# Attention probabilities transposed by VectorE in 32x32 blocks and DMA, with each group's queries projected one group ahead

## The chip, the cores and the metric

The kernel runs on one core of one Trainium2 chip. The metric is the device time of one launch in microseconds, the median of several runs. All data are fp32.

## What is computed

The input is a tensor of 2 images, 128 channels, 64 x 64 pixels. It goes through four layers: a state-space layer (layer 0), two attention layers over all 4096 pixels of an image (layers 1 and 2), and a multi-scale layer with attention over four scales at each pixel (layer 3). The change lies in layers 1 and 2, which are:

```
# layer 1: q, k, v are 3x3 convolutions of x, n = h * w = 4096
attn = softmax(einsum('bci,bcj->bij', q, k) * c ** -0.5, axis=2)
out  = einsum('bij,bcj->bci', attn, v).reshape(b, c, h, w)
x    = x + conv2d(out, Wo, bo, 0)
# layer 2: q, k, v are 1x1 projections of x
attn = softmax(einsum('nci,ncj->nij', q, k), axis=-1)
x    = gamma[0] * einsum('ncj,nij->nci', v, attn) + x
```

## The kernel before

Both images stay in SBUF the whole time, in `xt`, with channels on the 128 partitions and a border of zeros round each image. Layer 0 has an order of instructions written out by hand. From the attention layers on, the tile framework's scheduler chooses the order of each engine's instructions when the program is built, from the program's order and the buffers that each pool has. On every engine the instructions then run in that fixed order: one that waits holds back what stands behind it.

The two attention layers share the function `attention`, which is called once for each layer and image, four times in all. `project` and `finish` are given by the caller: `project` is the nine taps of a convolution in layer 1 (L633) and one product in layer 2 (L648); `finish` adds the result to `xt` (L638 after the output projection L637, or L651).

A call first projects the keys, the values and the queries of the whole image, 512 pixels at a time, into PSUM tiles `pp` of two chunks; ScalarE adds the bias and writes `k` and `q` (L572) or `vs` (L575). Values are transposed by PE (L579) and copied by VectorE (L581) to `vt`, which has keys on the partitions.

Then it goes through the queries in 16 groups of QG = 256, each in two blocks `it` of 128 queries:

- PE multiplies the block's queries with all keys (L594), into PSUM tiles `pq` of 1024 keys, of which there are two buffers. VectorE copies each to `sc` and takes the maximum on the way (L596).
- VectorE makes the negative scaled maximum `nm` (L598, L599), ScalarE takes the exponential of the whole row of 4096 in place and sums it (L601), and VectorE takes the reciprocal of the sum to `rec` (L602).
- `sc` has queries on the partitions, and the product with the values needs keys there. PE transposes it in 128 x 128 squares, four to a PSUM bank `ptt` (L607), and VectorE copies each bank to `pt` (L608). The eight `pt` tiles of a group have one of ten buffers each.
- When both blocks are there, PE sums the 32 products of `vt` with `pt` (L611) to `po`. The reciprocals are spread over the partitions by a product of ones with a diagonal matrix `dg` (L616, L617), copied by ScalarE to `rb` (L619), and multiplied in (L621).

The DMA queue of SyncE (SP) issues all transfers. In the attention layers it has only the loads of weights. DMAs are counted by eight semaphores in turn, so an issue waits until the DMA eight before it has landed. Each fp32 product is two passes of PE in the profile (so L594 counts 2048 and L611 4096 instructions); a transpose is one.

Of the kernel before, what the change touches and what calls it, by code (L numbers as in the profile page):

```python
# [6 lines left out]
F32 = mybir.dt.float32  # L7
AF = mybir.ActivationFunctionType
# [5 lines left out]
B, C, H, W = 2, 128, 64, 64  # L14
N = H * W
P = 128
CH = 512
NCH = N // CH
RPC = CH // W
# [39 lines left out]
WS_O, WS_Q, WS_K, WS_V, WS_IN, WS_OUT, WS_FUS = 0, 128, 256, 384, 512, 896, 1024  # L59
# [4 lines left out]
def tile_conv_seq(ctx: ExitStack, tc, x, consts, vecs, wemb, wlay, wconv, wdt, wqkv, wsmall, wms, out):  # L64
    nc = tc.nc
# [5 lines left out]
    ws = kp.tile([P, NWS], F32, name="ws")  # L71
    xt = kp.tile([P, B, H + 2, W + 2], F32, name="xt")
# [5 lines left out]
    def xv(b, c):  # L78

        return xt[:, b, 1 + c * RPC : 1 + (c + 1) * RPC, 1 : W + 1]  # L80
# [13 lines left out]
    ident = kc[:, K_ID : K_ID + P]  # L94
# [40 lines left out]
    with ExitStack() as s, tc.manual_schedule():  # L135
        wp = s.enter_context(tc.tile_pool(name="l0w", bufs=1))
        sp = s.enter_context(tc.tile_pool(name="l0s", bufs=1))
# [25 lines left out]
        for l in range(NL):  # L163
            w = wp.tile([P, NWL], F32, name=f"wl{l}")
# [12 lines left out]
            a = wp.tile([P, NJ, 4, 4], F32, name=f"am{l}")  # L177
            for g in range(4):
                pa = mm.tile([P, NJ, DS], F32, name="pa", tag="mm")
                nc.tensor.matmul(pa.rearrange("p j n -> p (j n)"), lhsT=four(g), rhs=an, start=True, stop=True)  # L180
                for q in range(4):
                    at = slice(32 * q, 32 * q + 32)
# [344 lines left out]
        for i in range(-2, NI + 2):  # L527
            todo = background(i)
            for t_ in range(NSL):
                t = i * NSL + t_  # L530
# [18 lines left out]
    wq = wbig.tile([P, 3, 9, C], F32, name="wq", tag="wbig")  # L549
    nc.sync.dma_start(wq, wqkv)  # L550
    nc.sync.dma_start(ws, wsmall)
    QG = 256
    with ExitStack() as s:
        sp = s.enter_context(tc.tile_pool(name="ats", bufs=1))
        pss = s.enter_context(tc.tile_pool(name="atps", bufs=2, space=PSUM))
        pst = s.enter_context(tc.tile_pool(name="atpt", bufs=2, space=PSUM))
        psa = s.enter_context(tc.tile_pool(name="atpa", bufs=1, space=PSUM))
        psm = s.enter_context(tc.tile_pool(name="atpm", bufs=1, space=PSUM))

        def attention(b, project, biases, scale, finish):  # L560

            q = sp.tile([P, N], F32, name="q", tag="q")
            k = sp.tile([P, N], F32, name="k", tag="k")
            vt = sp.tile([P, N // P, C], F32, name="vt", tag="vt")
            for which in (1, 2, 0):
                for c2 in range(NCH // 2):
                    pp = pss.tile([P, 2, CH], F32, name="pp", tag="s")
                    for i in range(2):
                        project(which, 2 * c2 + i, pp[:, i, :])
                    if which < 2:  # L570
                        dst = (q, k)[which][:, c2 * 2 * CH : (c2 + 1) * 2 * CH].rearrange("p (a f) -> p a f", a=2)
                        nc.scalar.activation(dst, pp, AF.Identity, bias=biases[which])  # L572
                        continue
                    vs = sp.tile([P, 2, CH], F32, name="vs", tag="vs", bufs=1)
                    nc.scalar.activation(vs, pp, AF.Identity, bias=biases[which])  # L575
                    for i in range(2):
                        pt = pst.tile([P, 4, P], F32, name="pvt", tag="t")
                        for a in range(4):
                            nc.tensor.transpose(pt[:, a, :], vs[:, i, a * P : (a + 1) * P], ident)  # L579
                        at = (2 * c2 + i) * 4  # L580
                        nc.vector.tensor_copy(vt[:, at : at + 4, :], pt)  # L581

            for grp in range(N // QG):
                pts = [sp.tile([P, 4, QG], F32, name="pt", tag="pt", bufs=10) for _ in range(NCH)]
                rec = sp.tile([P, 2], F32, name="rec", tag="rec", bufs=2)
                for it in range(QG // P):
                    qa = grp * QG + it * P
                    sc = sp.tile([P, N], F32, name="sc", tag="sc", bufs=3)
                    mx = sp.tile([P, NCH // 2], F32, name="mx", tag="mx", bufs=3)
                    for c2 in range(NCH // 2):  # L590
                        pq = pss.tile([P, 2, CH], F32, name="pq", tag="s")
                        for i in range(2):
                            at = (2 * c2 + i) * CH
                            nc.tensor.matmul(pq[:, i, :], lhsT=q[:, qa : qa + P], rhs=k[:, at : at + CH], start=True, stop=True)  # L594
                        dst = sc[:, c2 * 2 * CH : (c2 + 1) * 2 * CH].rearrange("p (a f) -> p a f", a=2)
                        nc.vector.tensor_scalar(dst, pq, 1.0, None, ALU.mult, ALU.max, accum_out=mx[:, c2 : c2 + 1])  # L596
                    nm = sp.tile([P, 1], F32, name="nm", tag="nm", bufs=3)
                    nc.vector.tensor_reduce(nm, mx, AX.X, ALU.max)  # L598
                    nc.vector.tensor_scalar(nm, nm, -scale, None, ALU.mult)  # L599
                    sm = sp.tile([P, 1], F32, name="sm", tag="sm", bufs=3)  # L600
                    nc.scalar.activation(sc, sc, AF.Exp, bias=nm, scale=scale, accum_out=sm)  # L601
                    nc.vector.reciprocal(rec[:, it : it + 1], sm)  # L602
                    for c in range(NCH):
                        pt = pst.tile([P, 4, P], F32, name="ptt", tag="t")
                        for a in range(4):
                            at = c * CH + a * P
                            nc.tensor.transpose(pt[:, a, :], sc[:, at : at + P], ident)  # L607
                        nc.vector.tensor_copy(pts[c][:, :, it * P : (it + 1) * P], pt)  # L608
                po = psa.tile([P, QG], F32, name="po", tag="acc")
                for jt in range(N // P):  # L610
                    nc.tensor.matmul(po, lhsT=vt[:, jt, :], rhs=pts[jt // 4][:, jt % 4, :], start=(jt == 0), stop=(jt == N // P - 1))  # L611

                pr = psm.tile([P, QG], F32, name="pr", tag="m")
                for it in range(QG // P):
                    dg = sp.tile([P, P], F32, name="dg", tag="dg", bufs=2)
                    nc.vector.tensor_scalar(dg, ident, rec[:, it : it + 1], None, ALU.mult)  # L616
                    nc.tensor.matmul(pr[:, it * P : (it + 1) * P], lhsT=ones, rhs=dg, start=True, stop=True)  # L617
                rb = sp.tile([P, QG], F32, name="rb", tag="rb", bufs=2)
                nc.scalar.copy(rb, pr)  # L619
                on = sp.tile([P, QG], F32, name="on", tag="on", bufs=2)  # L620
                nc.vector.tensor_tensor(on, po, rb, ALU.mult)  # L621
                finish(grp, on)

        def xg(b, grp):
            r = QG // W
            return xt[:, b, 1 + grp * r : 1 + (grp + 1) * r, 1 : W + 1]

        for b in range(B):
            def project(which, c, ps, b=b):
                for tap in range(9):  # L630
                    dy, dx = divmod(tap, 3)
                    rhs = xt[:, b, c * RPC + dy : (c + 1) * RPC + dy, dx : dx + W]
                    nc.tensor.matmul(ps, lhsT=wq[:, which, tap, :], rhs=rhs, start=(tap == 0), stop=(tap == 8))  # L633

            def finish(grp, on, b=b):
                p2 = psm.tile([P, QG], F32, name="p2", tag="m")
                nc.tensor.matmul(p2, lhsT=ws[:, WS_O : WS_O + C], rhs=on, start=True, stop=True)  # L637
                nc.vector.scalar_tensor_tensor(xg(b, grp), rows(p2), v1("bo1"), xg(b, grp), ALU.add, ALU.add)  # L638

            attention(b, project, [v1("bq1"), v1("bk1"), v1("bv1")], float(C) ** -0.5, finish)  # L640

        wm = wbig.tile([P, NS, 9, C], F32, name="wm", tag="wbig")
        nc.sync.dma_start(wm, wms)

        for b in range(B):
            def project(which, c, ps, b=b):
                at = WS_Q + which * C
                nc.tensor.matmul(ps, lhsT=ws[:, at : at + C], rhs=xv(b, c), start=True, stop=True)  # L648

            def finish(grp, on, b=b):  # L650
                nc.vector.scalar_tensor_tensor(xg(b, grp), rows(on), v1("gamma"), xg(b, grp), ALU.mult, ALU.add)  # L651

            attention(b, project, [v1("bq2"), v1("bk2"), v1("bv2")], 1.0, finish)


    with ExitStack() as s:
        sp = s.enter_context(tc.tile_pool(name="mss", bufs=1))
# [7 lines left out]
        for si in range(NS):  # L665
            for ti in range(NS):
                r = si * 32 + ti
# [3 lines left out]
        for b in range(B):  # L671
# [3 lines left out]
            for si in range(1, NS):  # L675
                sc_ = SCALES[si]
                hh = H // sc_
# [12 lines left out]
                for r0 in range(0, hh, rn):  # L690
                    pc = mm.tile([P, CH], F32, name="pcs", tag="mm")
                    pcv = pc[:, : rn * hh]
                    for tap in range(9):
                        dy, dx = divmod(tap, 3)
                        nc.tensor.matmul(  # L695
                            pcv, lhsT=wm[:, si, tap, :], rhs=xs[:, r0 + dy : r0 + dy + rn, dx : dx + hh],
# [8 lines left out]
                half = sc_ // 2  # L705
# [187 lines left out]
```

## Time and profile before

| | |
|---|---|
| median of 3 runs | 7203.03 us (7201.87 to 7207.1) |
| the profiled execution | 7203.93 us, its span 7202.1 us |
| mean granted PE clock | 0.912 |
| busy, share of the span | PE 93%, weight load 44%, VectorE 57%, ScalarE 32%, GpSimd 27% |
| layers 1 and 2, from the first `pp` to the last `xt` | 2743.8 to 5473.2 us |
| of these, PE busy | 2717.2 of 2729.4 us |
| DMA | 24.3 MB in the whole span |

A line of the page's part 5 gives a group of instructions: its line in the code, engine, operation, output and inputs, shape and count, then after the bar the busy time in us and the mean of one in ns, and after the second bar the time the engine stood idle just before them and what ended that. A line of instructions in order of time gives the start in us, the duration, engine, line, operation and count, and in brackets the idle time before and its releaser. [...] the distance of two starts tells what one costs in a row. The line PEclk gives the clock that PE was granted, in tenths of full speed, in 40 slices of the span.

### The profile page before, as it was taken

The page shows a single profiled execution, that of the slowest core. Times are in us where ns is not written, and L with a number is a line of the kernel's source. Part 1 is how long each engine was busy: PE and PEld are TensorE (multiplying, and loading weights), DVE is VectorE, ACT ScalarE, POOL GpSimd, SP SyncE. Part 2 cuts the span into 40 slices and gives each one's busy share as a digit, 9 for nine tenths or more (in the row PEclk, how much of TensorE's full clock was granted, in tenths as well). Part 3 has the DMA queues.
Part 4 walks back from the last instruction along what each step waited for, and adds up shares of the span by engine and source line. Part 5 has one row for each costly group of instructions (what it writes and reads, how often), then busy time and mean ns, then how long its engine had stood idle before and what let it go on. Part 6 is the DMA issues. An engine that isn't in the chain of part 4 may idle for free.

```text
span 7202.1 us, 51514 instructions
## 1 busy us (share of the span) xinstructions
PE 6665.2 (93%) x20224; PEld 3172.7 (44%) x20224; DVE 4083.1 (57%) x5497; ACT 2339.6 (32%) x2979; POOL 1924.5 (27%) x867
## 2 busy tenths in 40 slices
PE   7999999999999988999999999999998888888888
PEld 2222233222232223677557767776774333333333
DVE  5778878878778880466226656665663332332333
ACT  3565555555555551122112222222221111111111
POOL 3666666666666660000000000000001111111111
PEclk8888888888888889999999999999999888888888
DMA  1000000000000000000000000000000000000000
GB/s 49 0 0 0 0 3 3 5 2 0 0 0 3 3 3 12 1 1 1 0 14 1 1 1 1 1 1 1 1 1 0 3 2 3 3 2 3 3 3 3
DMA packets 22963, 24.30 MB, mean 3 GB/s; under 512 B 17456, under 2 KB 17600, under 8 KB 22464
## 3 DMA queue, kind: packets, MB, share of 16 engines
q1 hardware_dynamic: 22720, 21.01, 1.0%
q8 instruction: 159, 2.61, 0.2%
q14 instruction: 84, 0.69, 0.0%
HBM read 16.81 MB, written 4.19 MB: 3 GB/s over the span
## 4 chain that ended last, share of the span: by engine, by line
PE 55%; DVE 3%; POOL 2%; ACT 1%; issue 1%; DMA 0%; POOLq 0%; ACTq 0%; DVEq 0%; SPq 0%
PE po L611 12%; PE pq L594 12%; PE ptt L607 6%; PE pp L633 5%; PE po L791 4%; PE pw L788 4%; PE pqkv L742 2%; PE pf L722 2%; PE psc L756 2%; POOL prod L753 2%; PE pr L129 2%; PE pfus L801 1%; PE pcs L695 1%; PE pr L617 1%; PE pp L648 0%
## 5 line engine op out<-in xcount | busy, mean ns | idle before, releaser
L402 DVE TENSOR_TENSOR_SCAN h<-da,carry,h 128x512 f32<-128x512 f32 x1024 | 1271.7, 1270 | 269.8 <-ACT da L391 240.5
L405 POOL TENSOR_TENSOR h<-h,cb 128x2048 f32<-128x2048 f32 x256 | 1159.7, 4530 | 20.6
L601 ACT ACTIVATE sc<-sc,nm 128x4096 f32<-128x4096 f32 x128 | 475.0, 3711 | 1594.6 <-DVE nm L599 1594.6
L594 PE MATMUL pq<-k,q 128*128 128x512 f32 x2048 | 946.1, 593 | 0.0
L611 PE MATMUL po<-pt,vt 128*128 128x256 f32 x4096 | 926.8, 379 | 0.0
L391 ACT ACTIVATE da<-pdt,am 128x512 f32<-128x512 f32 x1024 | 673.0, 665 | 667.7 <-DVE h L402 635.3
L611 PEld LDWEIGHTS po<-pt,vt 128*128 128x128 f32 x4096 | 758.5, 190 | 92.5
L596 DVE TENSOR_SCALAR_CACHE_REDUCE sc<-pq 128x1024 f32<-128x1024 f32 x512 | 625.8, 1222 | 258.4 <-PE pq L594 257.6
L684 POOL MEMSET xs<- 128x1156 f32 (+2 forms) x6 | 3.4, 584 | 2802.5 <-DVE xt L651 2757.8
L608 DVE COPY pt<-ptt 128x512 f32<-128x512 f32 x1024 | 672.2, 685 | 40.6 <-PE ptt L607 38.4
L384 DVE TENSOR_TENSOR h<-bb,pdu 128x2048 f32<-128x2048 f32 x256 | 580.0, 2266 | 112.4 <-PE pdu L378 91.5
L753 POOL TENSOR_TENSOR prod<-qkv,qkv 128x2048 f32<-128x2048 f32 x64 | 286.9, 4505 | 1320.4 <-PE psc L756 1175.7
L607 PEld LDWEIGHTS ptt<-kc,sc 128*128 128x128 f32 x4096 | 478.5, 141 | 243.5 <-DVE pt L608 108.0
L607 PE MATMUL ptt<-kc,sc 128*128 128x128 f32 x4096 | 562.0, 274 | 9.2 <-ACT sc L601 9.2
L417 PE MATMUL py<-h,sel 128*32 128x512 f32 x2048 | 497.5, 629 | 1.5 <-POOL h L405 1.5
L594 PEld LDWEIGHTS pq<-k,q 128*128 128x128 f32 x2048 | 357.4, 190 | 298.0 <-issue 210.0
L366 PE MATMUL pb<-dbl,bsel 40*128 40x512 f32 x512 | 434.6, 983 | 17.3 <-ACT bb L367 16.0
L378 PE MATMUL pdu<-dtu,fsel 128*128 128x512 f32 x512 | 315.6, 702 | 90.7 <-DVE h L384 90.7
L633 PE MATMUL pp<-xt,wq 128*128 128x512 f32 x864 | 375.8, 595 | 5.4 <-DMA wq<-in_wqkv 5.4
L621 DVE TENSOR_TENSOR on<-po,rb 128x256 f32<-128x256 f32 x64 | 27.2, 424 | 617.0 <-PE po L611 604.5
L768 DVE TENSOR_REDUCE mx<-pst 128x128 f32<-128x512 f32 x16 | 11.1, 692 | 634.2 <-PE pst L764 634.2
L373 PE MATMUL pdt<-dt,fsel 128*128 128x512 f32 x512 | 334.8, 741 | 4.1 <-ACT da L391 3.8
(174 smaller groups left out, 7135.1 us busy)
## 6 DMA issues: line engine op xcount, KB each, us to landing
xt<-in_x SPq DMA_DIRECT2D x16, 256.0 KB, 4.9
xr<-in_x SPq DMA_DIRECT2D x16, 256.0 KB, 2.7
out<-ot SPq DMA_DIRECT2D x16, 256.0 KB, 2.0
wm<-in_wms SPq DMA_DIRECT2D x1, 2304.0 KB, 9.0
wl<-in_wlay SPq DMA_DIRECT2D x2, 936.0 KB, 7.7
wq<-in_wqkv SPq DMA_DIRECT2D x1, 1728.0 KB, 7.2
cw<-in_wconv SPq DMA_DIRECT2D x2, 512.0 KB, 8.4
ws<-in_wsmall SPq DMA_DIRECT2D x1, 768.0 KB, 5.3
```

The source lines that it names most:

```text
L384: nc.vector.tensor_tensor(h, st[i]["bc", 0], pdu.unsqueeze(1).to_broadcast([P, 4, CH]), ALU.mult)
L391: nc.scalar.activation(da, st[i]["pdt", s_], AF.Exp, scale=am[items[i][1]][:, j, gg, m : m + 1])
L402: nc.vector.tensor_tensor_scan(h[:, m, :], da, h[:, m, :], carries[b, l][:, j, gg, m : m + 1], ALU.mult, ALU.add)
L405: nc.gpsimd.tensor_tensor(h, h, st[i]["bc", 1], ALU.mult)
L417: nc.tensor.matmul(py[r : r + 32, :], lhsT=sel, rhs=st[i]["h", s_ + k][:, m, :], start=(m == 0), stop=(m == 3), tile_position=(0, r),)
L594: nc.tensor.matmul(pq[:, i, :], lhsT=q[:, qa : qa + P], rhs=k[:, at : at + CH], start=True, stop=True)
L596: nc.vector.tensor_scalar(dst, pq, 1.0, None, ALU.mult, ALU.max, accum_out=mx[:, c2 : c2 + 1])
L601: nc.scalar.activation(sc, sc, AF.Exp, bias=nm, scale=scale, accum_out=sm)
L607: nc.tensor.transpose(pt[:, a, :], sc[:, at : at + P], ident)
L608: nc.vector.tensor_copy(pts[c][:, :, it * P : (it + 1) * P], pt)
L611: nc.tensor.matmul(po, lhsT=vt[:, jt, :], rhs=pts[jt // 4][:, jt % 4, :], start=(jt == 0), stop=(jt == N // P - 1))
L633: nc.tensor.matmul(ps, lhsT=wq[:, which, tap, :], rhs=rhs, start=(tap == 0), stop=(tap == 8))
```

## The change

PE's transposes of `sc` and VectorE's copies of them go. In their place VectorE transposes each half of a row of keys (2048 of 4096) in blocks of 32 x 32 from `sc` to a tile `tr`. That leaves each block in the right orientation but on the partitions of its queries; 16 DMAs of 32 partitions x 2 KB carry the blocks from each quarter of the partitions to the quarter of their keys, in `pt`. They are 64 DMAs a group, all issued by SP. `pt` is now one tile for each half of the keys, in three buffers; `tr` has two buffers, which the values' `vs` shares. `sc` has two buffers where it had three.

The queries are no longer projected for the whole image: a function `query` projects one group of 256, into a bank of the pool that held the transposes, and is called one group ahead, ahead of the products with the values. `project` takes a start and a number of pixels for it. `rb` and `on` have one buffer where they had two.

```diff
-            q = sp.tile([P, N], F32, name="q", tag="q")
             k = sp.tile([P, N], F32, name="k", tag="k")
             vt = sp.tile([P, N // P, C], F32, name="vt", tag="vt")
-            for which in (1, 2, 0):
+            for which in (1, 2):
...
-                    vs = sp.tile([P, 2, CH], F32, name="vs", tag="vs", bufs=1)
+                    vs = sp.tile([P, 2, CH], F32, name="vs", tag="tr", bufs=2)
...
+            def query(grp):
+                pq = pst.tile([P, QG], F32, name="pqq", tag="t")
+                project(0, grp * QG, QG, pq)
+                q = sp.tile([P, QG], F32, name="q", tag="q", bufs=2)
+                nc.scalar.activation(q, pq, AF.Identity, bias=biases[0])
+                return q
+
+            q = query(0)
             for grp in range(N // QG):
-                pts = [sp.tile([P, 4, QG], F32, name="pt", tag="pt", bufs=10) for _ in range(NCH)]
+
+                pts = [sp.tile([P, QG // 32, NTH, 32], F32, name="pt", tag="pt", bufs=3) for _ in range(2)]
                 rec = sp.tile([P, 2], F32, name="rec", tag="rec", bufs=2)
                 for it in range(QG // P):
-                    qa = grp * QG + it * P
-                    sc = sp.tile([P, N], F32, name="sc", tag="sc", bufs=3)
+                    sc = sp.tile([P, N], F32, name="sc", tag="sc", bufs=2)
...
-                    for c in range(NCH):
-                        pt = pst.tile([P, 4, P], F32, name="ptt", tag="t")
-                        for a in range(4):
-                            at = c * CH + a * P
-                            nc.tensor.transpose(pt[:, a, :], sc[:, at : at + P], ident)
-                        nc.vector.tensor_copy(pts[c][:, :, it * P : (it + 1) * P], pt)
+                    for hh in range(2):
+                        tr = sp.tile([P, NB, NTH, 32], F32, name="tr", tag="tr", bufs=2)
+                        half = sc[:, hh * (N // 2) : (hh + 1) * (N // 2)]
+                        nc.vector.transpose(tr, half.rearrange("p (t r f) -> p r t f", r=NB, f=32))
+                        for turn in range(NB):
+                            for ib in range(NB):
+                                r = (ib + turn) % NB
+                                nc.sync.dma_start(
+                                    pts[hh][32 * r : 32 * r + 32, it * NB + ib, :, :], tr[32 * ib : 32 * ib + 32, r, :, :]
+                                )
+                if grp + 1 < N // QG:
+                    q = query(grp + 1)
                 po = psa.tile([P, QG], F32, name="po", tag="acc")
                 for jt in range(N // P):
-                    nc.tensor.matmul(po, lhsT=vt[:, jt, :], rhs=pts[jt // 4][:, jt % 4, :], start=(jt == 0), stop=(jt == N // P - 1))
+                    nc.tensor.matmul(po, lhsT=vt[:, jt, :], rhs=pts[jt // NTH][:, :, jt % NTH, :], start=(jt == 0), stop=(jt == N // P - 1))
...
-                rb = sp.tile([P, QG], F32, name="rb", tag="rb", bufs=2)
+                rb = sp.tile([P, QG], F32, name="rb", tag="rb")
...
-                on = sp.tile([P, QG], F32, name="on", tag="on", bufs=2)
+                on = sp.tile([P, QG], F32, name="on", tag="on")
```

with `NB, NTH = P // 32, N // P // 2`, so 4 and 16. The two `project` functions get the arguments `at, n` (a start and a number of pixels) and take their rows of `xt` from these.

More of the change, by code (lines that the diff above doesn't have):

```diff
@@ L552, in tile_conv_seq @@
     QG = 256
+    NB, NTH = P // 32, N // P // 2
     with ExitStack() as s:
@@ L568, in attention @@
                     for i in range(2):
-                        project(which, 2 * c2 + i, pp[:, i, :])
+                        project(which, (2 * c2 + i) * CH, CH, pp[:, i, :])
                     if which < 2:
-                        dst = (q, k)[which][:, c2 * 2 * CH : (c2 + 1) * 2 * CH].rearrange("p (a f) -> p a f", a=2)
+                        dst = k[:, c2 * 2 * CH : (c2 + 1) * 2 * CH].rearrange("p (a f) -> p a f", a=2)
                         nc.scalar.activation(dst, pp, AF.Identity, bias=biases[which])
                         continue
-                    vs = sp.tile([P, 2, CH], F32, name="vs", tag="vs", bufs=1)
+                    vs = sp.tile([P, 2, CH], F32, name="vs", tag="tr", bufs=2)
                     nc.scalar.activation(vs, pp, AF.Identity, bias=biases[which])
@@ L593, in attention @@
                             at = (2 * c2 + i) * CH
-                            nc.tensor.matmul(pq[:, i, :], lhsT=q[:, qa : qa + P], rhs=k[:, at : at + CH], start=True, stop=True)
+                            nc.tensor.matmul(pq[:, i, :], lhsT=q[:, it * P : (it + 1) * P], rhs=k[:, at : at + CH], start=True, stop=True)
                         dst = sc[:, c2 * 2 * CH : (c2 + 1) * 2 * CH].rearrange("p (a f) -> p a f", a=2)
@@ L628, in tile_conv_seq, with project @@
         for b in range(B):
-            def project(which, c, ps, b=b):
+            def project(which, at, n, ps, b=b):
                 for tap in range(9):
                     dy, dx = divmod(tap, 3)
-                    rhs = xt[:, b, c * RPC + dy : (c + 1) * RPC + dy, dx : dx + W]
+                    rhs = xt[:, b, at // W + dy : (at + n) // W + dy, dx : dx + W]
                     nc.tensor.matmul(ps, lhsT=wq[:, which, tap, :], rhs=rhs, start=(tap == 0), stop=(tap == 8))
@@ L645, in tile_conv_seq, with project @@
         for b in range(B):
-            def project(which, c, ps, b=b):
-                at = WS_Q + which * C
-                nc.tensor.matmul(ps, lhsT=ws[:, at : at + C], rhs=xv(b, c), start=True, stop=True)
+            def project(which, at, n, ps, b=b):
+                w = WS_Q + which * C
+                rhs = xt[:, b, 1 + at // W : 1 + (at + n) // W, 1 : W + 1]
+                nc.tensor.matmul(ps, lhsT=ws[:, w : w + C], rhs=rhs, start=True, stop=True)
             def finish(grp, on, b=b):
```

## The prediction

> **What bounds the kernel now.** I read the page first, then the stretches of the two attention stages, then PE's and VectorE's instructions in order of time inside one group of 256 queries. From the page, the busy tenths, PE's granted clock and the four groups that make up a group of queries:
>
> ```profile
> PE   7999999999999988999999999999998888888888
> PEclk8888888888888889999999999999999888888888
> L594 PE MATMUL pq<-k,q 128*128 128x512 f32 x2048 | 946.1, 593 | 0.0
> L611 PE MATMUL po<-pt,vt 128*128 128x256 f32 x4096 | 926.8, 379 | 0.0
> L607 PE MATMUL ptt<-kc,sc 128*128 128x128 f32 x4096 | 562.0, 274 | 9.2 <-ACT sc L601 9.2
> L608 DVE COPY pt<-ptt 128x512 f32<-128x512 f32 x1024 | 672.2, 685 | 40.6 <-PE ptt L607 38.4
> ```
>
> PE is full in the attention slices and waits before none of these lines. The stretches by stage (one image's 16 groups of layer 1, then of layer 2; the columns are PE, weight load, VectorE, ScalarE, POOL, clock) say the same at full clock, with VectorE at 60%:
>
> ```profile
> 2935.70:3520.30 584.60, 584.29 (x2675) 411.05 (x2674) 351.23 (x672) 128.75 (x81) 0.00 (x0) 1.00 0.00 1
> 4284.40:4877.90 593.50, 591.01 (x2707) 413.80 (x2706) 355.64 (x681) 140.67 (x92) 0.00 (x0) 1.00 0.00 1
> ```
>
> A group's period is the distance of two long runs of `po` in the chain: 3363.09 − 3326.99 = 36.10 us in layer 1, 4618.71 − 4583.28 = 35.43 us in layer 2 (no output projection there). The pieces, by PE's instructions in order of time:
>
> ```profile
> 3340.46 1.02 PE L594 MATMUL pq<-k,q 128*128 128x512 f32 x2
> 3341.32 1.04 PE L607 MATMUL ptt<-kc,sc 128*128 128x128 f32 x8
> 3342.19 1.02 PE L594 MATMUL pq<-k,q 128*128 128x512 f32 x2
> ```
>
> Eight transposes take 3342.19 − 3341.32 = 0.87 us of PE, two score passes 0.86 us. So a 128-column pass is 0.108 us, a 256-column one 0.216, a 512-column one 0.429 (fp32 products take two passes, transposes one), and a score tile of 1024 keys (four passes) is 1.72 us. The softmax's turn-around, all engines:
>
> ```profile
> 3315.08 0.15 DVE L599 TENSOR_SCALAR nm<-nm 128x1 f32<-128x1 f32 x1
> ...
> 3315.33 3.71 ACT L601 ACTIVATE sc<-sc,nm 128x4096 f32<-128x4096 f32 x1 [22.74 <-DVE nm L599]
> ...
> 3319.16 0.16 DVE L602 RECIPROCAL rec<-sm 128x1 f32<-128x1 f32 x1 [0.65 <-ACT sc L601]
> ```
>
> VectorE's reciprocal stands in its queue behind `nm` and waits until the Exp and its accumulator are through, 3.9 us later. Today PE has transposes and `po` passes to run meanwhile.
>
> [...] PE's first convolution passes after 9.1 us of idle, and the same shape without a gap in the chain:
>
> ```profile
> 5480.84 18.62 PE L695 MATMUL pcs<-xs,wm 128*128 128x512 f32 x36 [9.10 <-DVE xs L685]
> ```
>
> Warm, 36 such passes take 15.46 us (`pp` at 2842.91), so the idle cost 3.2 us more; after the 5.42 us idle at 2743.81 36 passes took 18.38, 2.9 us more. Gaps of 1.3 and 2.3 us at 5560 and 5565 left no slow passes behind. [...] No 32x32 transpose is in this trace; the row with as many elements is `h` (L384), 128x2048 in 2.27 us. [...]
>
> **The change part by part, per group.**
>
> *PE, removed:* 64 transposes x 0.108 = 6.96 us. *Moved:* the query projection, 8 chunks x 9 taps x 2 passes x 0.429 = 61.8 us an image, becomes 18 passes x 0.216 = 3.9 us a group (layer 2: 2 x 0.216 = 0.43), as much in sum. So before, with queries, a group is 39.96 and 35.86 us; PE's remaining work is 33.0 and 28.9.
>
> *VectorE:* 16 copies at 0.60 (pairs in 1.28) = 9.6 us go; four block transposes come. I take 2.27 us each, from L384[...]. Each also waits for eight DMA semaphores, which no row shows: 0 to 0.6 us (eight times the smallest VectorE step, 0.08), I take 0.3. Sum 10.3 us: VectorE's load hardly moves, but its order does.
>
> *DMA:* 64 pieces of 64 KB, all on SP. At the kernel's start SP's issues follow each other at 0.39 to 0.47 us:
>
> ```profile
> 12.11 0.43 SPq L167 DMA_DIRECT2D cw<-in_wconv  x1
> 12.58 0.38 SPq L169 DMA_DIRECT2D wd<-in_wdt  x1
> 13.01 0.34 SPq L165 DMA_DIRECT2D wl<-in_wlay  x1
> 13.40 0.93 SPq L167 DMA_DIRECT2D cw<-in_wconv  x1
> ```
>
> At 0.43 that is 27.5 us a group[...]. Each issue waits for the DMA eight before it; 256 KB pieces land 2.0 to 2.7 us after issue (page, part 6), less than 8 x 0.43 = 3.4. So I count SP at nothing: 27.5 us beside more than 40. If that cover is gone it is the third rival.
>
> *The new wait.* With the transposes gone from PE, only two PSUM tiles of scores stand between PE and VectorE. In VectorE's order in the changed program (layer 1), between the evacuation that frees the last tile of one 128-query block and the next block's first evacuation stand: evacuation 1.14, transpose 0.3 + 2.27, `nm` pair 0.5, the reciprocal waiting for that block's own Exp 3.9, reciprocal and `dg` 0.4, second transpose 0.3 + 2.27, evacuation 1.2: 12.3 us. PE covers two tiles of it, 2 x 1.72 − 0.2 = 3.2. It idles 9.1 us a group. In layer 2 one transpose stands before that evacuation; PE idles 1.6 + 6.9 us with a `pr` of 0.3 inside, net 8.2. The second block's same chain lies behind the 13.8 us of `po`, and costs nothing. Both exceed what the trace shows to drop the clock (4.3 to 9.1 us): 3.0 us more, the mean of 2.9 and 3.2.
>
> Sum: layer 1 33.0 + 9.1 + 3.0 = 45.1 against 39.96, +5.1; layer 2 28.9 + 8.2 + 3.0 = 40.1, and about 0.3 for restarts, 40.4 against 35.86, +4.6. Times 32 each: 163 + 147 = +310. At each image's ends one stall is missing (4 x 12 = 48) and filling the pipeline adds about 5 (20), an estimate: −28. Net +282. The profiled execution has a span of 7202.1 and 1.8 around it, 7203.9, 0.9 above the median of the runs: 7203 + 282 = 7485. *Small edits:* `rb`, `on`, `sc`, `vs` on fewer buffers hide behind the same idle (up to 0.5 us a group if not); `po` reading runs of 32 instead of 256: the projection's `xt` rows of 64 already run at 0.429.
>
> **Rivals.** First, the same idle without the clock's drop (the `pr` in layer 2's gap[...]): 7485 − 64 x 3.0 = 7293. For it: 2.3 us gaps stay warm. Against: 4.3 us and more never do.
>
> Second, the block transpose runs at half rate: two on the chain, 2 x 2.2 x 64 = +282: 7767. Nothing in the trace speaks for it.
>
> Third, the transfers set the pace. Beyond 45.1 / 64 = 0.70 us a piece (layer 2: 0.63) the SP queue is the bound. At 0.8 a group is 51.2: 32 x 11.2 + 32 x 15.3 = +848, so 8050. The first `xt` loads did take 8.76 / 8 = 1.1 us each, at 256 KB a piece; at 1.1 a group would be 70.4, and the time 9280. Against: those move four times the bytes.
>
> Fourth, on the other side: faster, if PE's idle stays under the 6.96 us that the transposes took, at full clock. [...] 2 x 1.12 + 0.6 = 2.8 us less, idle 6.3 and 5.4 (5.7 with the restarts), a gain of 0.7 and 1.3 a group: 7203 − 32 x 2.0 − 28 = 7111. It decides at an idle of 7.0 us, and only if such idle leaves the clock alone, which the trace denies.
>
> That the change doesn't do what it says is excluded: no PE transpose of `sc` is left in the changed program.
>
> **How the numbers follow.** Likeliest, idle and half clock: 0.62, own range 7390 to 7560 (waits 0 to 0.6 on two transposes: about ±40, [...]ends ±28). Full clock 0.12, half-rate transposes 0.08, transfers 0.10, faster 0.08. The range runs from 7270 to 7790: it leaves out the transfers and the gain, 0.18. Faster by over 0.2% 0.08, within 0.2% 0.02, slower 0.90; 0.2% is about what a measurement of this kernel can tell from no change.
>
> **What would show it.** PE idle before `pq`, released by VectorE's `sc`, 8 to 9 us once a group, some 550 us in all; VectorE idle before `rec`, released by ScalarE's `sc`, 3 us each; PE's clock in the attention slices down to 0.85 to 0.95; score passes of 0.86 us after each gap; block transposes of 2.3 us; SP issues 0.43 apart with idle between the blocks. If PE waits before `po` for DMA, or SP issues without a pause, the transfers were under-priced; if no gap of over 5 us shows, the order was misread.

## The result, and the profile after

The changed kernel takes 7522.88 us (median of 4 runs, 7521.9 to 7524.01) against 7203.23 of the kernel before in the same session: a ratio of 1.0443 with a 95% interval of 1.0425 to 1.0461, so 320 us slower. The prediction was 7485. All but some 5 us of the loss lies in the two attention stages: the first normalization `on` starts at 2949.0 us instead of 2977.7, the last one at 5787.7 instead of 5472.2.

From the page after, first PE's and its clock's tenths, then the groups that answer to those shown of before (line, engine, operation, count, busy time and mean, idle time ahead and who ended it), and the transfers (KB, us from issue to landing):

```profile
PE   7999999999999988888978777777776888888888
PEclk8888888888888899899988988989887898889888
L604 PE MATMUL pq<-k,q 128*128 128x512 f32 x2048 | 1068.1, 673 | 456.4 <-DVE sc L606 456.4
L627 PE MATMUL po<-pt,vt 128*128 128x256 f32 x4096 | 915.3, 382 | 65.5 <-DMA pt<-tr 60.7
L616 DVE STREAM_TRANSPOSE tr<-sc 128x2048 f32<-128x2048 f32 x256 | 591.0, 2310 | 371.6 <-DMA pt<-tr 361.7
pt<-tr SPq DMA_DIRECT2D x4096, 64.0 KB, 2.0
```

PE now waits 456 us before score passes, and its clock falls in the attention slices; in stretches of layer 1 and layer 2 it is granted 0.90 and 0.88 (third figure from the end; 1.00 before):

```profile
3000.00:3600.00 600.00, 487.64 (x1629) 314.33 (x1629) 273.11 (x384) 111.11 (x78) 0.00 (x0) 0.90 0.40 95
4500.00:5000.00 500.00, 384.05 (x1242) 241.09 (x1241) 256.55 (x363) 103.57 (x73) 0.00 (x0) 0.88 0.43 102
```

That is what the prediction described. The same gap in the order of time, in layer 1, on PE and then on VectorE:

```profile
3342.86 5.32 PE L604 MATMUL pq<-k,q 128*128 128x512 f32 x12
3356.69 10.19 PE L604 MATMUL pq<-k,q 128*128 128x512 f32 x16 [8.51 <-DVE sc L606]
3366.71 3.62 PE L627 MATMUL po<-pt,vt 128*128 128x256 f32 x16
```

```profile
3345.93 2.31 DVE L616 STREAM_TRANSPOSE tr<-sc 128x2048 f32<-128x2048 f32 x1
3348.16 0.11 DVE L608 TENSOR_REDUCE nm<-mx 128x1 f32<-128x4 f32 x1
3348.31 0.15 DVE L609 TENSOR_SCALAR nm<-nm 128x1 f32<-128x1 f32 x1
3352.39 0.16 DVE L612 RECIPROCAL rec<-sm 128x1 f32<-128x1 f32 x1 [3.93 <-ACT sc L611]
3352.59 0.28 DVE L632 TENSOR_SCALAR dg<-kc,rec 128x128 f32<-128x128 f32 x1
3352.96 2.31 DVE L616 STREAM_TRANSPOSE tr<-sc 128x2048 f32<-128x2048 f32 x1
3355.40 1.22 DVE L606 TENSOR_SCALAR_CACHE_REDUCE sc<-pq 128x1024 f32<-128x1024 f32 x1
```

The reciprocal waits 3.93 us for Exp, with a transpose and the next eviction behind it, and PE stands still for 8.51 us. A reader could stop here. But SP's queue, which the prediction counted at nothing, shows another thing. Its issues in 45 us of layer 2, and the two things that it waited for longest from 2900 to 5800 us (us in total, times, longest):

```profile
4699.75 45.39 SPq L620 DMA_DIRECT2D pt<-tr  x70
```

```profile
SPq L620 <- DVE tr L616: 196.3, 3, 128.4
SPq L620 <- DVE nm L609: 47.4, 20, 3.7
```

There are 256 block transposes. The three waits that bear their name fall between one call of `attention` and the next. The 20 waits put down to `nm` all lie in layer 1, and they too are waits for a transpose: in the gap shown above SP goes on at 3348.27, 0.03 us after the transpose of 3345.93 has ended. So SP catches up with VectorE now and then in layer 1, 47.4 us in 32 groups or 1.5 us a group, and in layer 2 it issues without a pause: 45.39 / 70 = 0.648 us a piece, so the 64 pieces of a group take 41.5 us. A group (the distance of two `on`, mean over an image's 16) takes 43.5 and 42.8 us in layer 1, 41.5 and 41.3 in layer 2: SP's 41.5, and in layer 1 its pauses on top. In the chain that ended last, 16% of the span now stands under SP's issues, which have no share in it before:

```profile
PE 35%; SPq 16%; DVE 6%; issue 2%; DMA 2%; POOL 2%; ACT 1%; DVEq 0%; POOLq 0%; ACTq 0%
```

So two causes are left. **Theory V** (the prediction's): VectorE's queue, where the reciprocal's wait for Exp and the transposes hold evictions back. **Theory S** (its third rival): the pace of SP's issues. In layer 1 the trace shows some of both. They differ in what helps.

### The profile page after: what moved, and what is told of

Read it like the earlier page. It is cut to its first block, busy times and chain, and to the rows that moved or that the text cites. A ratio compares the mean times of both kernels' runs of the same rounds, so it can differ in the third digit from the quotient of the medians.

```text
span 7522.2 us, 49321 instructions
## 1 busy us (share of the span) xinstructions
PE 6382.5 (85%) x16448; PEld 2872.9 (38%) x16448; DVE 4034.4 (54%) x4729; ACT 2351.2 (31%) x3027; POOL 1924.3 (26%) x867
## 4 chain that ended last, share of the span: by engine, by line
PE 35%; SPq 16%; DVE 6%; issue 2%; DMA 2%; POOL 2%; ACT 1%; DVEq 0%; POOLq 0%; ACTq 0%
SPq L620 16%; PE po L627 7%; PE pq L604 6%; PE po L808 3%; PE pw L805 3%; PE pp L649 3%; PE pqkv L759 2%; DVE tr L616 2%; PE pf L739 2%; PE psc L773 2%; POOL prod L770 2%; PE pr L129 2%; DMA pt<-tr 2%; PE pfus L818 1%; DVE sc L606 1%
## 5 line engine op out<-in xcount | busy, mean ns | idle before, releaser
L604 PE MATMUL pq<-k,q 128*128 128x512 f32 x2048 | 1068.1, 673 | 456.4 <-DVE sc L606 456.4
L627 PEld LDWEIGHTS po<-pt,vt 128*128 128x128 f32 x4096 | 782.5, 192 | 209.1 <-issue 101.6
L604 PEld LDWEIGHTS pq<-k,q 128*128 128x128 f32 x2048 | 431.2, 217 | 991.4 <-DVE sc L606 592.1
L616 DVE STREAM_TRANSPOSE tr<-sc 128x2048 f32<-128x2048 f32 x256 | 591.0, 2310 | 371.6 <-DMA pt<-tr 361.7
L635 ACT COPY rb<-pr 128x256 f32<-128x256 f32 x64 | 23.8, 372 | 921.4 <-PE pr L633 529.0
L807 DVE TENSOR_TENSOR ov<-qkv,pw 128x512 f32<-128x512 f32 x256 | 175.9, 687 | 251.5 <-PE pw L805 246.4
L805 PE MATMUL pw<-at,spread 128*128 128x512 f32 x512 | 271.0, 655 | 10.8 <-ACT at L798 10.8
L808 PE MATMUL po<-ov,ws 128*128 128x512 f32 x512 | 270.7, 654 | 0.0
```

The costliest lines, as they stand in the source:

```text
L604: nc.tensor.matmul(pq[:, i, :], lhsT=q[:, it * P : (it + 1) * P], rhs=k[:, at : at + CH], start=True, stop=True)
L616: nc.vector.transpose(tr, half.rearrange("p (t r f) -> p r t f", r=NB, f=32))
L627: nc.tensor.matmul(po, lhsT=vt[:, jt, :], rhs=pts[jt // NTH][:, :, jt % NTH, :], start=(jt == 0), stop=(jt == N // P - 1))
L805: nc.tensor.matmul(pw, lhsT=spread[:, si, ti, :], rhs=at_, start=True, stop=True)
L808: nc.tensor.matmul(po, lhsT=ws[:, WS_OUT : WS_OUT + C], rhs=ov, start=(ti == 0), stop=(ti == NS - 1))
```

## The experiments

**1. The reciprocal off VectorE's queue, half of the pieces off SP's, both, and a third score tile.** Four kernels from the changed one. The first scales `dg` by the sum instead of its reciprocal, on ScalarE, and inverts the spread sums:

```diff
-                    nc.vector.reciprocal(rec[:, it : it + 1], sm)
+                    sms.append(sm)
...
-                    nc.vector.tensor_scalar(dg, ident, rec[:, it : it + 1], None, ALU.mult)
+                    nc.scalar.activation(dg, ident, AF.Identity, scale=sms[it])
...
-                nc.scalar.copy(rb, pr)
+                nc.vector.reciprocal(rb, pr)
```

> The reciprocal leaves VectorE's queue behind the Exp: ScalarE makes dg from the sum itself, and VectorE takes the reciprocal of the spread sums pr. Theory 1 (VectorE's queue is held by its wait for the Exp, and PE idles behind it): the chain loses 3.9 us, PE's idle before pq falls from about 8.5 to under 5 us a group, the time falls by 64 x 3.9 = 250 to about 7270, further if PE's clock stays up (64 x 3.0 = 190 more). Theory 2 (SP's issues at about 0.62 us set the period: 64 x 0.62 = 40 us a group): layer 1 can fall from 44 to about 41 us at most, layer 2 stays at 41.7; 7420 to 7520.

Measured: 7485.03 us, ratio 1.0392 [1.0375, 1.0409], 38 us less than the changed kernel. The wait for Exp is gone from VectorE, and what stands in its place is the wait for transfers (total, times, longest; 361.7 us in the changed kernel):

```profile
DVE tr L616 <- DMA pt<-tr: 696.4, 177, 9.1
PE pq L604 <- DVE sc L606: 401.3, 146, 8.9
```

A group in layer 1 falls to 42.0 us (mean of 42.3 and 41.7), and is 41.4 and 41.2 in layer 2, nearly as before. SP's pauses put down to `nm` fall from 47.4 to 2.8 us. So the reciprocal's wait accounts for about a tenth of the loss, nearly all of it in layer 1; the transposes still stand in VectorE's queue.

The second changes one line, where the pieces are issued:

```diff
-                                nc.sync.dma_start(
+                                (nc.sync if turn % 2 == 0 else nc.gpsimd).dma_start(
```

> Half of the 64 DMAs of each group are issued by GpSimd, idle in these layers, in place of SP. Theory 1: only the transposes' waits for DMA go (1.3 us a group in layer 2, little in layer 1): about 7470, PE's idle before pq stays at 8 to 9 us in layer 1. Theory 2: SP's 40 us become 20 and the period falls until the next bound, PE with its idle at 37 to 38 us: 7150 or below.

Measured: 7021.89 us, ratio 0.9751 [0.9736, 0.9766]: 501 us less than the changed kernel, and faster than the kernel before. PE's waits before scores are 32.9 us instead of 456.4, with the reciprocal still in VectorE's queue. SP now waits for transposes 121 times (in the changed kernel 23 times, with the waits put down to `nm`):

```profile
L604 PE MATMUL pq<-k,q 128*128 128x512 f32 x2048 | 991.7, 633 | 32.9 <-DVE sc L606 32.9
SPq L620 <- DVE tr L616: 1007.8, 121, 145.9
```

The third does both edits.

> Both edits: no wait for the Exp in VectorE's queue, and half of the DMAs on GpSimd. If the two bounds stand side by side (theory 1 with SP close behind), this gains far more than the two alone: PE's work of 33 and 29 us a group plus an idle of 3 to 5: 64 x about 5 below the 44 and 41.7 of now, and the clock's part: about 7000, below the kernel before. Theory 1 alone: as the first edit alone. Theory 2 alone: as the second edit alone.

Measured: 7053.4 us, ratio 0.9791 [0.9777, 0.9806]. With the pieces split, moving the reciprocal gains nothing more; the time is 31 us longer.

The fourth gives scores a third PSUM tile, so that PE covers more of a hold-up in VectorE's queue (`pvt` and `pqq` go to the pool of `pr`):

```diff
-        pss = s.enter_context(tc.tile_pool(name="atps", bufs=2, space=PSUM))
-        pst = s.enter_context(tc.tile_pool(name="atpt", bufs=2, space=PSUM))
+        pss = s.enter_context(tc.tile_pool(name="atps", bufs=3, space=PSUM))
```

> A third PSUM buffer for the score tiles (the value transposes and the queries move to the pool of pr). Theory 1: PE covers one tile more, 1.7 us a group less idle: 64 x 1.7 = 110 less, about 7410, less of it in layer 2 where SP is close behind. Theory 2: no change, 7500 to 7520.

Measured: 7509.42 us, ratio 1.0425 [1.0409, 1.044]. PE's wait before scores falls by 148 us and its wait before `po` for transfers grows by 124:

```profile
L603 PE MATMUL pq<-k,q 128*128 128x512 f32 x2048 | 983.2, 636 | 308.7 <-DVE sc L605 304.2
L626 PE MATMUL po<-pt,vt 128*128 128x256 f32 x4096 | 958.1, 394 | 192.1 <-DMA pt<-tr 185.1
```

The same idle time under another name. So far all speaks for S. But the split's 501 us is not clean: with other queues the scheduler also chose another order of PE's and VectorE's instructions (transposes in pairs behind an Exp that is long done, `po` in one run of 64 passes).

**2. The same order for both.** In two more kernels the attention's order is written out by hand, once with all pieces on SP and once split; within the groups both programs have the same instructions in the same order on PE and VectorE. The core of the loop for group `grp`: `pieces` is the scores and evictions of a block's tiles that are named last, `exps` is `nm` and Exp, `turned` is the reciprocal, `dg`, two transposes and their pieces (first of block 1 of the group before, then of block 0 of this one), and `po` and `on` of the group before come at the end:

```
pieces(q, 0, *bl[0], (0,))
finish(*pend)
pieces(q, 0, *bl[0], (1,))
dg1 = turned(1, lsc, lsm, lpts)
pieces(q, 0, *bl[0], (2, 3))
sm0 = exps(*bl[0])
...
q1 = query(grp + 1)
pieces(q, 1, *bl[1], (0, 1))
dg0 = turned(0, bl[0][0], sm0, pts)
pieces(q, 1, *bl[1], (2, 3))
sm1 = exps(*bl[1])
...
```

> The attention's order is written out by hand (block transposes after the other block's first two evictions, the reciprocal where its Exp is long done, po after both blocks' scores), and all 64 pieces of a group stay on SP. If the pace of SP's queue is the bound (64 pieces at 0.59 to 0.62 us, 38 to 40 us in each of 64 groups, against 42 to 44 in the changed kernel), the better order buys little: 7330 to 7500 us, and SP issues without a pause. If instead the other order of instructions, which came along when half of the pieces went to GpSimd, was what made that kernel fast, this one gets it too, with SP alone: 7000 to 7100 us.

Measured: 7489.9 us, ratio 1.0399 [1.0384, 1.0415]. A better order with SP alone is worth 33 us. Its groups take 41.8, 41.6, 41.5 and 41.2 us in the four calls: the same in layer 1 and layer 2, although PE has 4.1 us less to do in layer 2. SP's issues in 45 us, the duration of one (min/median/max in ns), and a gap that PE still has before scores:

```profile
3299.88 45.17 SPq L621 DMA_DIRECT2D pt<-tr  x70
L621 SPq DMA_DIRECT2D pt<-tr x4096: 507/588/1798, 2898.0 to 5745.0; - x196
3338.12 9.30 PE L597 MATMUL pq<-k,q 128*128 128x512 f32 x16 [5.84 <-DVE sc L599]
```

45.17 / 70 = 0.645 us from issue to issue, times 64 is 41.3 us: the group's length.

> The same order by hand as the kernel with all pieces on SP, line by line, but the pieces of odd turns are issued by GpSimd. If the pace of one queue is the bound, this alone is worth 300 to 500 us against that kernel: 6980 to 7060 us, with TensorE busy nearly throughout. If the order is what counts, the two differ by less than 50 us.

Measured: 6957.8 us, ratio 0.9659 [0.9644, 0.9673]. The queue alone, at the same order, is worth 532 us, a little more than expected; groups take 32.4 us in layer 1 and 33.4 in layer 2. PE has no gap to speak of in this part of layer 1, and the 16 passes of scores that took 9.30 us behind a gap (10.19 in the changed kernel) take 7.13:

```profile
3301.51 4.05 PE L680 MATMUL pqq<-xt,wq 128*128 128x256 f32 x18
3305.62 7.13 PE L597 MATMUL pq<-k,q 128*128 128x512 f32 x16
3312.59 13.98 PE L662 MATMUL po<-pt,vt 128*128 128x256 f32 x64
3326.41 1.88 PE L597 MATMUL pq<-k,q 128*128 128x512 f32 x4
```

**3. Issues or bytes?** Two kernels with the order by hand and all pieces on SP. The first moves half of each piece's bytes, with as many issues:

```diff
-  pts[hh][32 * r : 32 * r + 32, it * NB + ib, :, :], tr[32 * ib : 32 * ib + 32, r, :, :]
+  pts[hh][32 * r : 32 * r + 32, it * NB + ib, : NTH // 2, :], tr[32 * ib : 32 * ib + 32, r, : NTH // 2, :]
```

> The order by hand with all 64 pieces on SP, but each piece moves only half of its bytes (1 KB instead of 2 KB of each of 32 partitions); the second product reads the moved half twice, so half of the weights are left out. If SP's pace is a price for each issue, the time stays within 60 us of the kernel with whole pieces. If it is the bytes, by which the queue fills and holds the next issue, it falls to 6980 to 7100 us.

Measured: 7503.3 us, ratio 1.0417 [1.0401, 1.0432]. Half of the bytes save nothing; the time is 13 us longer. In the same stretch of layer 1 the DMA engines' share (second figure from the end) halves, first with whole pieces, then with half of them:

```profile
2900.00:3550.00 650.00, 545.52 (x1837) 354.72 (x1838) 320.98 (x461) 128.44 (x93) 0.00 (x0) 0.92 0.43 102
```

```profile
2900.00:3550.00 650.00, 537.09 (x1818) 350.30 (x1818) 321.27 (x461) 127.33 (x92) 0.00 (x0) 0.92 0.21 51
```

The second keeps the bytes written and halves the issues:

```diff
-                        for ib in range(NB):
+                        for ib in range(0, NB, 2):
...
-  pts[hh][32 * r : 32 * r + 32, it * NB + ib, :, :], tr[32 * ib : 32 * ib + 32, r, :, :]
+  pts[hh][32 * r : 32 * r + 32, it * NB + ib : it * NB + ib + 2, :, :],
+  tr[32 * ib : 32 * ib + 32, r : r + 1, :, :].broadcast_to([32, 2, NTH, 32]),
```

> The order by hand, all pieces on SP, but half as many: 32 for a group, each of which writes one block of the weights to two neighbouring places, so that bytes and rows written stay the same. Half of the transposed weights are left out and others stand twice in their place. If SP's pace is a price for each issue (0.645 us each), SP needs 20.6 us for a group, less than TensorE's 29 to 33, and the time is that of the split kernel or a little less: 6920 to 7000 us. If the price goes with the rows or bytes that are written, it stays near the whole pieces on SP: 7400 to 7500 us.

Measured: 6912.43 us, ratio 0.9596 [0.9582, 0.9611], with no second queue at all, so it is not GpSimd that makes the split kernels fast. A group takes 32.2 to 33.5 us. An issue that writes 128 KB lasts as long as one of 64 KB (median 596 against 588 ns), and SP waits for transposes again:

```profile
L621 SPq DMA_DIRECT2D pt<-tr x2048: 585/596/2156, 2902.2 to 5164.8; - x187
SPq L621 <- DVE tr L617: 1037.0, 128, 161.7
```

From 32 to 128 KB the price is one for each issue: 0.641, 0.645 and 0.641 us at 32, 64 and 128 KB. Theory S stands, and bandwidth is not what it is about.

**4. The other half of the change alone.** The kernel before, with its transposes on PE, and only the queries projected a group ahead, as the change does it:

```diff
+                if grp + 1 < N // QG:
+                    q = query(grp + 1)
                 po = psa.tile([P, QG], F32, name="po", tag="acc")
```

> The kernel before with only the second part of the change: queries are projected a group ahead, the transposes stay on TensorE. The prediction counted this part as work moved and nothing added: 7185 to 7235 us. If the 9 passes of 256 columns at the end of a group cost more than the passes of 512 they replace, or break TensorE's run, 7240 to 7300 us.

Measured: 7647.25 us, ratio 1.0619 [1.0601, 1.0636]. Neither expectation: 444 us slower. PE in a group of layer 1:

```profile
3115.95 12.18 PE L604 MATMUL pq<-k,q 128*128 128x512 f32 x28
...
3133.33 1.25 PE L617 MATMUL ptt<-kc,sc 128*128 128x128 f32 x8 [0.19 <-DVE pt L618]
3137.88 1.97 PE L617 MATMUL ptt<-kc,sc 128*128 128x128 f32 x8 [3.30 <-ACT sc L611]
```

All score passes of the group come first, and between the second block's Exp and its transposes no scores of the next group are left to run, because their queries stand behind these transposes in the program. PE waits 3.30 us there, and its clock from 2900 to 3550 us is 0.93 instead of 1.00. One more kernel has the projection at the head of the group:

```diff
             for grp in range(N // QG):
+                if grp + 1 < N // QG:
+                    qn = query(grp + 1)
...
-                    q = query(grp + 1)
+                    q = qn
```

> Queries a group ahead alone, with TensorE's transposes as in the kernel before, but projected ahead of the group's scores and not behind its transposes. TensorE's order is then again the one of the kernel before, with eight score passes of the next group between the last Exp and its transposes. If the 444 us that the queries cost alone came from the place in the order (4.4 us of waiting for Exp and evictions in each group, and passes at a lower clock behind it), the time goes back to 7190 to 7240 us. If the projection in pieces of 256 columns costs it, it stays near 7600 us.

Measured: 7210.34 us, ratio 1.0009 [1.0, 1.0018]: all but 7 us are back. PE is busy 649.70 of 650 us at full clock:

```profile
2900.00:3550.00 650.00, 649.70 (x2947) 462.64 (x2946) 339.54 (x649) 132.68 (x94) 0.00 (x0) 1.00 0.00 1
```

The projection itself costs next to nothing; its place in the program cost 437 us. What this place costs in the changed kernel was not run. It has the queries there too, but SP's 41.3 us a group stand beside whatever PE does; with the pieces split by one line and the queries in the same place, a group of layer 1 takes 33.7 us, close to PE's 33.0.

**5. The fastest.** Split pieces, and an order by hand in which all evictions of a group come first, three of its four transposes lie beside `po`, and the fourth behind the next group's first eviction (`tr` on three buffers; `turned` is one transpose with its pieces, `share` the reciprocal and `dg`, and `po` of the group before stands where the lower of the two middle lines is left out):

```
pieces(q, 0, *bl[0], (0,))
turned(1, 1, lsc, lpts)
...
pieces(q, 0, *bl[0], (1, 2, 3))
sm0 = exps(*bl[0])
pieces(q, 1, *bl[1], (0, 1, 2, 3))
sm1 = exps(*bl[1])
q = query(grp + 1)
...
dg0 = share(sm0)
turned(0, 0, bl[0][0], pts)
turned(0, 1, bl[0][0], pts)
dg1 = share(sm1)
turned(1, 0, bl[1][0], pts)
...
```

> The candidate for the fastest: pieces split over SP and GpSimd, and another order by hand. All evictions of scores come first, and three of a group's four block transposes lie beside the 32 passes of po (12.2 us), the fourth behind the next group's first eviction; tr has three buffers. If what is left in the split kernel (about 200 us over the 6758 us that the kernel before less 64 times 6.96 us gives) is TensorE waiting for evictions that stand behind two transposes, it falls to 6780 to 6880 us. If it is the pieces' landing or TensorE's clock, it stays at 6930 to 7000 us.

Measured: 6868.64 us, ratio 0.9535 [0.9519, 0.955], the fastest of all, 89 us under the other order. In layer 1 a group takes 32.9 us (32.4 with the other order), in layer 2 it falls from 33.4 to 30.0; a stretch of layer 2 with the other order, then with this one (PE first, clock third from the end):

```profile
4400.00:5000.00 600.00, 533.26 (x1797) 341.03 (x1795) 355.67 (x517) 148.99 (x110) 264.51 (x543) 0.95 0.45 119
```

```profile
4400.00:5000.00 600.00, 561.81 (x1994) 368.57 (x1993) 398.14 (x575) 163.77 (x121) 297.05 (x608) 0.99 0.49 133
```

PE's longest wait for an eviction in layer 2 falls from 5.0 to 1.7 us. So once SP is out of the way, evictions that stand behind transposes seem to cost, as theory V has it, though in layer 2 alone. This is not shown by itself: PE's order and the buffers of `tr` and `rb` changed together with VectorE's order.

## Why the prediction came out as it did

The time, the sign and most of the marks in the profile were right (not SP's issues, which were to be 0.43 us apart with idle between the blocks). The cause put behind them holds for a part of layer 1 only; what bound the rest was counted at nothing. That the number came within 38 us is luck.

- *PE, 6.96 us of transposes removed, 33.0 and 28.9 us left:* about right. With the pieces split, groups take 32.4 us in layer 1 and, in the best order, 30.0 in layer 2.
- *A block transpose at 2.27 us:* right, 2.31. The second rival falls.
- *PE's new idle of 9.1 us and 3.0 us at a lower clock behind it:* seen as described (8.51 us; 16 passes in 10.19 instead of 7.13 us; 456 us in all against some 550), so the first rival falls too. The 3.0 was rightly taken from the trace: after the 9.10 us of idle in the kernel before, PE is granted a clock of 0.50 from 5480.84 to 5486.5 us and 1.00 from 5487, and its 36 passes take 18.62 − 15.46 = 3.16 us more; after the 8.51 us in the changed kernel it is 0.50 from 3356.6 to 3362.5 us, with score passes 0.85 us apart, and 1.00 from 3363, with passes 0.43 apart. In the trace of before the clock is 0.50 within 0.3 us after every gap of 4.0 us and more; after 13 of the 14 gaps of 2.33 or 2.34 us it is 1.00, after the one at 6421.85 us 0.50. But the idle is not what sets the pace. Removing the reciprocal's wait moved 38 us of 320, because most of PE's idle is time that SP would have used anyway.
- *"So I count SP at nothing: 27.5 us beside more than 40":* the step that failed, by a term that was mis-sized. 0.43 us came from three steps between weight loads at the kernel's start; the excerpt's fourth line, an issue of 0.93 us, was left out. These pieces go from issue to issue in 0.645 us, so 41.3 us a group. The reason against the third rival, that the dearer `xt` loads move four times the bytes, does not carry over: 32, 64 and 128 KB cost SP 0.641, 0.645 and 0.641 us here. With 0.645 in the prediction's own sums, the third rival's threshold for layer 2 (0.63) is passed and that for layer 1 (0.70) is not. In layer 2 SP's 41.3 takes the place of 40.4 (measured 41.4). In layer 1 the sum of 45.1 stays above it, but was 1.9 too long: measured are 43.2, nearly all of them SP's 41.5 and the 1.5 in which SP waits for VectorE.
- *Landing in 2.0 to 2.7 us:* the page before also has 4.9 us, for the `xt` loads of the same 256 KB. The pieces landed in 2.0 (4.0 at the longest), less than the 8 x 0.645 = 5.2 us of eight issues, so the eight semaphores did not hold SP, as the prediction said.
- *Why the number held:* by luck, the two causes cost nearly the same here. Against 39.96 and 35.86 the measured groups are +3.2 and +5.5 instead of +5.1 and +4.6 (4.5, by its own sum); times 32 each, +279 instead of +310. By subtraction the remaining 41 us of the 320 lie outside the groups, nearly all at the ends of the images, where −28 was predicted; that was not followed up.
- *The projection "moved", at no price:* right for the work (7 us), and wrong as a reason not to look at its place: alone, where the change puts it, it costs 444 us.
- *The fourth rival, faster:* it was rightly improbable for this kernel, but its condition was wrong. It was put on block transposes 1.12 us shorter than 2.27 and on no waits in VectorE's queue; split by one line, the kernel is faster with transposes of 2.30 us and the reciprocal still in that queue. What decides first is that SP's issues stay under PE's 33.0 and 28.9 us, so under 0.52 and 0.45 us a piece (an estimate), or go over two queues. Then the change gains 182 us (the split alone) to 334 us (the best order).
- *What stays open:* how long the changed kernel would take in its own order with SP out of the way, since the scheduler gave the split kernel another order; and why these pieces cost SP more than the weight loads.

With 64 pieces of 64 KB a group, the issue time on SP was the bound (41.3 us a group), and sharing it out over two queues gave 532 us.

## What to carry to other kernels

Price a transfer's issue from a transfer of the same kind, multiply by the count, and compare the sum with the length of the stage; a queue that hardly ever waits for its producer (SP 23 times for 256 block transposes) is the first suspect, whatever the other engines' waits are called. A long wait that the trace names is not yet a cause: take it away, and see whether the same idle time comes back under another name. When two variants differ in a queue, look whether the scheduler has also given them another order, and write the order out by hand to compare them.

## What was not expected of the hardware

- A piece from one quarter of the partitions to a quarter costs SP 0.64 to 0.65 us from issue to issue, whether it writes 32 KB (45.52 us for 71), 64 KB (45.17 for 70) or 128 KB (8.33 for 13); the first four weight loads in the prediction's excerpt follow each other at 0.39 to 0.47.
- With two queues GpSimd issues the same pieces in 0.497 us each (the split by one line), and a piece lands in 2.6 to 2.8 us (median of a queue, split by one line and by hand) instead of 2.0, at up to 133 GB/s in a stretch (the fastest kernel, layer 2). No slowing of VectorE's transposes beside them shows (2.30 us against 2.31).
